# Graph layer on one core: runs grouped by ten neighbouring node tiles, with degrees, scales and parts following each group

## The chip, the cores and the metric

The kernel runs on one core of one Trainium2 chip. The metric is the device time of one execution in microseconds. Before the change it is 1150.8 us as the median of three executions (1150.80, 1148.29 and 1150.85). The profile is of one further execution, which took 1151.31 us.

TensorE multiplies matrices, VectorE and ScalarE work on rows of 128 partitions, GpSimd (POOL) here mostly issues indirect transfers, and SyncE (SP) issues plain ones. Each engine works through its own queue of instructions.

## The reference

A graph with 6250 nodes and 206250 directed edges (sorted by destination, self loops among them) is given with node features x of 256 columns.

```python
x = x + gnn(layernorm(x), edges)          # eps 1e-5
x = x + ffn(layernorm(x))

def gnn(v):                                # own loops are added once more
    deg  = segment_sum(1, dst)             # edges into each node, plus one
    dinv = 1 / sqrt(deg)
    h    = v @ W
    out  = segment_sum(h[src] * dinv[src] * dinv[dst], dst) + b
    return where(out > 0, out, a * out)

def ffn(v):                                # mixture of 8 experts, 2 chosen for the whole sequence
    ...                                    # gelu(v @ W1 + b1) @ W2 + b2, weighted, then layernorm
```

The degrees come out of the edge list, which is sorted by destination: the edges of two neighbouring nodes (a pair, one run) lie side by side.

## The kernel before

The 6250 nodes are padded to 49 tiles of 128 (NT = 49), and to 3200 pairs of neighbouring nodes (NPR). The kernel has three stages.

**The prelude** (lines 200 to 589). x is loaded in seven blocks of seven tiles (`x_load`). One h step (`h_step`) takes two tiles: four transposes on TensorE, a copy to SBUF on ScalarE (`xT`), and, one step later, eight passes of matmul with the weight, whose result ScalarE copies into `hk`. There are 25 double tiles, so 26 steps. Per-row statistics of x come from VectorE (`x_stats`, one block of seven tiles at a time), and the reciprocal root of the variance from them (`dm`, `va`, `rs`).

Meanwhile the edges are sorted into runs. A packed copy of the edge list, key and low bits of the source, goes to DRAM (`pk_d`). A coarse count (lines 324 to 337) tells where a window of 512 edges must start, `search(w)` finds the exact start of each run in it, and POOL fetches the runs with indirect transfers: 25 of them, in five groups of WP = 5 (NW = 5). Each brings one run to each of the 128 partitions. Run number c on partition p is pair 25 p + c, so group w holds pairs 25 p + 5 w to 25 p + 5 w + 4 of every partition: a group is spread over all nodes. `keys(w)` subtracts the run's base on VectorE, `turn_keys(w)` transposes on TensorE and ScalarE copies the result into `keyT` and `loT` (pair along the columns, edge slot along the partitions). `key_hots(w)` compares on VectorE and writes, interleaved, a one for each edge into the pair's first node and a one for each edge into its second node (`ev`, lines 499 and 500).

Only when all five groups are there can degrees be counted: 49 matmuls of `ev` with ones (line 545), then deg, dinv and the scale sc = rs * dinv for all 49 tiles at once. `parts(n)` then writes the scaled h of tile n as a high part (ScalarE, line 563) and the rest as a low part (VectorE, line 564) into `hp`. Three tiles' parts are placed inside each of the last six h steps, the others after h's end, among the first work of the node loop. `keep(i)` (line 784) stores seven tiles of parts to DRAM (`hl_d`) on SP.

Also in the prelude: `one_hots(u)` on VectorE makes the one-hot rows of 16 pairs from loT and keyT (lines 455), with two buffers named `unit`, which the groups of runs use as well.

**The node loop** (lines 795 to 866). For node tile n, `counts` turns one-hots into a 49 x 128 x 128 count tile `a_t` on TensorE (line 624), copied by ScalarE (line 628), and `sums` multiplies it with all 49 tiles of parts (line 644): 39 tiles this way; the last ten are summed by gathering rows of `hl_d` (lines 737 and 775). `node` and `stat` are the epilogue. Tile 0's counts and sums and tile 1's counts are written out ahead of the loop.

**Routing and the feed-forward part** (from line 929) follow the last node.

The order of the instructions on all five engines in the first two stages is the program's own (a manual schedule): an instruction waits in its queue behind those written ahead of it. SBUF is shared by slots: `s0` holds the packed edges, `s1` the loaded edges, `s2` to `s5` the blocks of x, `s6` holds `ev`; the seven blocks of parts take the same slots later.

Of the kernel before, what the change touches and what calls it, by code (L numbers as in the profile page):

```python
# [24 lines left out]
P = 128  # L25
# [9 lines left out]
def gnn_moe_kernel(  # L35
# [92 lines left out]
    WA = 3  # L128
    HG = 16
# [5 lines left out]
    assert HG * (P + PK) // 2 >= WP * P * 2  # L135
# [56 lines left out]
    with ExitStack() as ph:  # L192
# [38 lines left out]
        def x_load(i):  # L231

            if i % 2 == 0:
                x_two[0] = slots.tile([P, 2, TB, D], F32, name="xb", tag=f"s{2 + i // 2}")
            xb = x_two[0][:, i % 2]
            full = min(TB, N // P - i * TB)
            r0 = i * TB * P
            nc.sync.dma_start(
                out=xb[:, :full, :],
                in_=x[r0 : r0 + full * P, :].rearrange("(t p) d -> p t d", p=P),  # L240
            )
            for t in range(full, TB):
                for p0, r0, r in node_rows(i * TB + t):
                    nc.sync.dma_start(out=xb[p0 : p0 + r, t, :], in_=x[r0 : r0 + r, :])
            xbs[i] = xb

# [10 lines left out]
        nc.gpsimd.iota(g_i, pattern=[[1, NW], [NW, P]], base=0, channel_multiplier=0)  # L257
# [7 lines left out]
        make_identity(nc, ident_0)  # L265
        q_i = ep.tile([P, NC], I32, name="q_i")
        nc.gpsimd.iota(q_i, pattern=[[2, NC]], base=0, channel_multiplier=2 * NC)
# [150 lines left out]
        def search(w):  # L418
# [18 lines left out]
            runs[w] = unit()[:, : WP * P * 2].rearrange("p (j e f) -> p j e f", j=WP, f=2)  # L437
# [28 lines left out]
        ev = slots.tile([P, NPR, 2], BF16, name="ev", tag=f"s{NB_T - 1}")  # L466
# [11 lines left out]
        def turn_keys(w):  # L478
            key = kts.pop(w)
            s = slice(w * WP, (w + 1) * WP)  # L480
            lo = runs[w].rearrange("p j e f -> p j (e f)").bitcast(BF16)
            lo = lo.rearrange("p j (e f) -> p j e f", f=4)
            pks = [ps_k.tile([P, WP, P], BF16, name=f"pk{i}") for i in range(2)]
            for j in range(WP):
                nc.tensor.transpose(pks[0][:, j, :], key[:, j, :], ident_b)
            for j in range(WP):

                nc.tensor.transpose(pks[1][:, j, :], lo[:, j, :, 3], ident_b)
            for v, pk_ in ((keyT, pks[0]), (loT, pks[1])):
                nc.scalar.copy(  # L490
                    v.rearrange("s (p c) -> s p c", c=NC)[:, :, s],
                    pk_.rearrange("s c p -> s p c"),
                )

        def key_hots(w):
            s = slice(w * WP, (w + 1) * WP)
            k = keyT.rearrange("s (p c) -> s p c", c=NC)[:, :, s]
            e = ev.rearrange("s (p c) j -> s p c j", c=NC)[:, :, s, :]
            nc.vector.tensor_scalar(e[:, :, :, 0], k, float(NT), None, op0=OP.is_lt)
            nc.vector.scalar_tensor_tensor(  # L500
                e[:, :, :, 1], k, float(2 * NT), e[:, :, :, 0], op0=OP.is_lt, op1=OP.subtract
            )

        for i in range(2, NB_T):
            x_load(i)
        h_some(2)
# [8 lines left out]
        search(3)  # L515
        h_some(1)
        search(4)
        x_stats(2)
        h_room(1)
        hk.append((2 * HK, 1, hk2))  # L520
        h_some(2)

        dm = ep.tile([P, NT], F32, name="dm")
        va = ep.tile([P, NT], F32, name="va")
        for w in range(NW):
            keys(w)
            turn_keys(w)
            if w + 3 < NB_T:
                x_stats(w + 3)
            if w + 4 == NB_T:  # L530
                nc.vector.tensor_tensor(dm, st[:, :, 1], st[:, :, 4], OP.subtract)
                nc.vector.tensor_tensor(va, st[:, :, 2], st[:, :, 5], OP.add)
                nc.vector.scalar_tensor_tensor(dm, dm, 0.25, dm, op0=OP.mult, op1=OP.mult)
                nc.vector.scalar_tensor_tensor(va, va, 1.0 / D, dm, op0=OP.mult, op1=OP.add)
                nc.vector.tensor_scalar(va, va, LN_EPS, None, op0=OP.add)
                nc.scalar.activation(rs, va, AF.Sqrt)
            if w + 1 == NW:
                nc.vector.reciprocal(rs, rs)
            h_some(2 if w + 1 < NW else 1)
            key_hots(w)  # L540


        pdeg = pcnt[:, NW : NW + NT]
        for n in range(NT):
            nc.tensor.matmul(
                pdeg[:, n : n + 1],
                ev[:, n * P // 2 : (n + 1) * P // 2, :].rearrange("s i j -> s (i j)"), ones_b,
                start=True, stop=True, skip_group_check=True,
            )
        deg = ep.tile([P, NT], F32, name="deg")  # L550
        nc.vector.tensor_scalar(deg, pdeg, 1.0, None, op0=OP.add)
        nc.scalar.activation(dinv, deg, AF.Sqrt)
        nc.vector.reciprocal(dinv, dinv)
        nc.vector.tensor_tensor(sc, rs, dinv, OP.mult)

        def parts(n):
            i, t = divmod(n, TB)
            if t == 0:
                hp2[i] = slots.tile([P, TB, 2, D], F32R, name=f"hp{i}", tag=f"s{i}")
            h = h_at(n)[:, 0, :]  # L560
            s = sc[:, n : n + 1]
            hi, lo = (hp2[i][:, t, k, :] for k in range(2))
            nc.scalar.activation(hi, h, AF.Copy, scale=s)
            nc.vector.scalar_tensor_tensor(
                lo, h, s, hi.bitcast(F32), op0=OP.mult, op1=OP.subtract
            )

        ns = iter(range(NT))
        def some_parts(k):
            for n in itertools.islice(ns, k):  # L570
                parts(n)

        made = 0
        while h_some(1, lambda: some_parts(3)):
            made += 1
            if made in (3, 5):
                one_hots(made // 4)
# [13 lines left out]
    with main:  # L591
# [189 lines left out]
        for n in range(3):  # L781
            load(n)

        def keep(i):
            nc.sync.dma_start(
                out=hl_d[i * TB * P : (i + 1) * TB * P, :].rearrange("(t p) d -> p t d", p=P),
                in_=hp2[i].rearrange("p t k d -> p t (k d)").bitcast(F32),
            )
# [4 lines left out]


        kept, summed = 0, 0
        for n in ns:
            parts(n)
            if n % TB == TB - 1 or n == HK + 2:
                for kept in range(kept, (n + 1) // TB):
                    keep(kept)  # L800
                kept = (n + 1) // TB
            if n == HK + 2:
                counts_of(0, 0)
                counts_of(0, 1)
                one_hots(2)
            if n == HK + 5:
                counts_of(0, 2)
                one_hots(3)
            if n == HK + 7:
                counts_of(0, 3)  # L810
            if n > HK + 7:

                sums(0, summed, n)
                summed = n
# [3 lines left out]
        sums(0, summed, NT)  # L818
        for c in range(NHG):
            counts_of(1, c)  # L820
            one_hots(NHG + 2 + c) if c < 3 else None
        for g in range(3):
            g_edges(g)
# [521 lines left out]
```

## Time and profile before

| what | value |
|---|---|
| median of three executions | 1150.8 us |
| profiled execution, own time | 1151.31 us |
| its span | 1149.2 us |
| TensorE busy | 1090.8 us (95%) |
| VectorE busy | 721.5 us (63%) |
| ScalarE busy | 623.1 us (54%) |
| POOL busy | 539.0 us (47%) |
| first transposes of x | 14.03 us |
| the five groups' keys start | 41.35, 46.33, 51.70, 58.01, 64.91 us |
| all degrees on TensorE | 69.40 us |
| end of h | 82.35 us |
| first sums of tile 0 | 98.25 us |
| first counts of tile 2 (the loop) | 118.72 us |
| last sums | 765.6 us |

Times in the timeline are microseconds from the span's start, and a row names the engine, the line of the code, the operation, and the tiles written and read, followed by sizes and types. In brackets stands how long the engine sat idle ahead of the instruction and what ended that. PEclk is the share of TensorE's full clock that was granted. Busy time of an engine is not a bound by itself: an engine may be waiting in its queue while work further back in it is ready.

### The profile page before, as it was taken

To read this page: it belongs to the slowest core of one execution; us is meant where nothing else is said; L and a number is where in the kernel's file an instruction comes from. 1 tells how busy PE (TensorE), PEld (TensorE's weight loads), DVE (VectorE), ACT (ScalarE), POOL (GpSimd) and SP (SyncE) were. 2 spreads that over 40 slices of the span, in tenths; PEclk is the share of its full clock that TensorE was granted. 3 is DMA by queue.
4 is the path that set the end of the run, shared out by engine and by line. 5 is a ranking of instruction groups with operands and counts; after the bars stand their busy time and mean duration, and the time that the engine had idled before them with its cause. 6 is when DMAs were issued, how large, how long until landed. Compare 5 with 4: busy or idle time off the path is not lost. (4 is left out here: it accounts for less than half of the span.)

```text
span 1149.2 us, 17869 instructions
## 1 busy us (share of the span) xinstructions
PE 1090.8 (95%) x6552; PEld 836.3 (73%) x6552; DVE 721.5 (63%) x1523; ACT 623.1 (54%) x1529; POOL 539.0 (47%) x473
## 2 busy tenths in 40 slices
PE   6977999999999999999999999885999999999997
PEld 5766788878888888788888888763566666666666
DVE  6878876867777877777777778745333333322335
ACT  3786466766766666676667666522533333333330
POOL 3713246777767676777666766425411111100000
PEclk9997899999999999999999999886999999999999
DMA  8709637676767777677777777534011111100001
GB/s 261 237 24 343 196 86 198 160 189 172 196 172 185 179 174 182 176 180 180 184 177 177 180 182 174 140 92 140 23 37 37 37 37 37 37 19 18 19 19 37
DMA packets 102750, 152.04 MB, mean 132 GB/s; under 512 B 10047, under 2 KB 48671, under 8 KB 102655
## 3 DMA queue, kind: packets, MB, share of 16 engines
q0 software_dynamic: 54080, 99.35, 35.3%
q1 hardware_dynamic: 45378, 48.93, 13.0%
q10 hardware_dynamic: 3196, 2.55, 0.8%
q8 instruction: 53, 0.87, 0.3%
q14 instruction: 43, 0.34, 0.1%
HBM read 123.42 MB, written 27.37 MB: 131 GB/s over the span
## 5 line engine op out<-in xcount | busy, mean ns | idle before, releaser
L737 POOL DMA_INDIRECT rows<-hl_d,g_src x360 | 409.5, 1137 | 221.7 <-PE pg L775 104.6
L644 PE MATMUL po<-hp,a_t 128*128 128x512 f32 x1911 | 481.8, 402 | 0.8 <-ACT a_t L628 0.8
L644 PEld LDWEIGHTS po<-hp,a_t 128*128 128x128 f32 x1911 | 351.9, 190 | 70.2 <-ACT a_t L628 1.0
L628 ACT CAST a_t<-pa 128x392 fp32r<-128x392 f32 x624 | 257.8, 502 | 218.0 <-PE pa L624 216.5
L455 DVE TENSOR_TENSOR unit<-iota,loT 128x2048 bf16<-128x2048 bf16 x156 | 190.4, 1221 | 51.3 <-PE pa L624 51.3
L1261 PE MATMUL p<-xT,w_sb 128*128 128x512 f32 (+2 forms) x416 | 173.0, 577 | 1.6 <-ACT xT L917 1.6
L1282 PE MATMUL p<-w_sb,hT 128*128 128x256 f32 (+1 forms) x784 | 171.2, 379 | 0.0
L1282 PEld LDWEIGHTS p<-w_sb,hT 128*128 128x128 f32 (+1 forms) x784 | 147.9, 190 | 20.8 <-issue 0.9
L624 PEld LDWEIGHTS <-unit 128*128 128x128 bf16 x2496 | 124.1, 100 | 49.0 <-issue 24.8
L624 PE MATMUL pa<-unit 128*128 128x98 bf16 x2496 | 148.6, 212 | 9.5 <-DVE unit L455 5.6
L455 DVE TENSOR_TENSOR unit<-iota,keyT 128x1568 bf16<-128x1568 bf16 x156 | 150.8, 967 | 0.0
L1261 PEld LDWEIGHTS p<-xT,w_sb 128*128 128x128 f32 x416 | 79.6, 200 | 88.2 <-issue 82.9
L1287 DVE TENSOR_TENSOR yt<-yt,p 128x256 f32<-128x256 f32 (+1 forms) x49 | 20.6, 421 | 179.6 <-PE p L1282 179.6
L756 ACT ACTIVATE oh_g<-iota_f,g_dst 128x128 fp32r<-128x128 f32 x360 | 123.9, 423 | 0.0
L1265 ACT ACTIVATE hT<-p,b_sb 128x512 f32<-128x512 f32 (+2 forms) x104 | 67.3, 660 | 82.9 <-PE p L1261 82.7
L775 PE MATMUL pg<-rows,oh_g 128*128 128x512 f32 x360 | 106.0, 392 | 1.6 <-DMA rows<-hl_d,g_src 1.6
L1292 ACT ACTIVATE rs<-rs 128x1 f32<-128x1 f32 (+1 forms) x49 | 9.9, 203 | 150.0 <-DVE rs L1291 150.0
L925 POOL TENSOR_TENSOR xt<-xt,beta_bc 128x1024 f32<-128x1024 f32 (+1 forms) x13 | 29.5, 2274 | 130.0 <-DVE yt L910 130.0
L775 PEld LDWEIGHTS pg<-rows,oh_g 128*128 128x128 f32 x360 | 68.1, 189 | 18.4 <-DMA rows<-hl_d,g_src 3.7
L922 POOL TENSOR_TENSOR yt<-yt,b_sb 128x1024 f32<-128x1024 f32 (+1 forms) x13 | 29.6, 2273 | 89.7 <-PE px L915 80.4
L758 ACT ACTIVATE oh_g<-oh_g 128x384 fp32r<-128x384 f32 (+1 forms) x140 | 67.1, 479 | 4.4
L679 DVE RECIPROCAL rstd<-rstd 128x1 f32<-128x1 f32 (+1 forms) x49 | 8.0, 164 | 88.2 <-ACT rstd L678 88.2
(183 smaller groups left out, 777.1 us busy)
## 6 DMA issues: line engine op xcount, KB each, us to landing
hl_d<-hp SPq DMA_DIRECT2D x7, 1792.0 KB
x_d<-x SPq DMA_DIRECT2D x49, 128.0 KB
xt<-x_d SPq DMA_DIRECT2D x12, 512.0 KB
out_dram<-yt SPq DMA_DIRECT2D x48, 128.0 KB
rows<-hl_d,g_src POOLq DMA_INDIRECT x360, 3.8
xb<-in_x_dram SPq DMA_DIRECT2D x6, 896.0 KB
xs<-in_x_dram SPq DMA_DIRECT2D x39, 128.0 KB
xg<-in_x_dram SPq DMA_DIRECT2D x9, 128.0 KB
```

What stands on the lines that cost most here:

```text
L455: nc.vector.tensor_tensor(oh, iota2[:, :m, :].unsqueeze(1).to_broadcast([P, HG // 2, m, 2]), v[:, s].rearrange("p (q t) -> p q t", t=2).un ...
L624: nc.tensor.matmul(pa[:, i].rearrange("p j h -> p (j h)"), oh_lo[:, q, :, t], oh_key[:, q, :, t], start=True, stop=True,)
L628: nc.scalar.copy(tiles[n][:, :, b * 2 * BG : (b + 1) * 2 * BG], pa.rearrange("p i j h -> p h (i j)"),)
L644: nc.tensor.matmul(pouts[n].rearrange("p k d -> p (k d)"), tiles[n][:, g, :], hp2[g // TB][:, g % TB].rearrange("p k d -> p (k d)"), start ...
L737: nc.gpsimd.indirect_dma_start(out=g_rows[j], out_offset=None, in_=hl_d, in_offset=bass.IndirectOffsetOnAxis(ap=g_src[:, j // GC, j % GC : ...
L756: nc.scalar.activation(oh[:, i, :], iota_f, AF.Abs, bias=g_neg[:, g, c : c + 1])
L758: nc.scalar.activation(oh, oh.bitcast(F32), AF.Relu, scale=-1.0, bias=1.0)
L775: nc.tensor.matmul(pouts[n].rearrange("p k d -> p (k d)"), oh[:, i, :], g_rows.pop(g * GC + c), start=False, stop=(c == GC - 1),)
L922: nc.gpsimd.tensor_tensor(yt[:, :nt, :], yt[:, :nt, :], b2_sb.unsqueeze(1).to_broadcast([P, nt, D]), OP.add)
L1261: nc.tensor.matmul(p1[:, :cols], w1_sb[:, e, k, f * P : (f + 1) * P], xT[:, k, :cols], start=(k == 0), stop=(k == ND - 1),)
L1265: nc.scalar.activation(hT[:, e, f, :cols], p1[:, :cols], AF.Gelu, bias=b1_sb[:, e, f : f + 1])
L1282: nc.tensor.matmul(p2[:r], hT[:, e, f, t * P : t * P + r], w2_sb[:, e, f, :], start=(e == 0 and f == 0), stop=(e == TOP_K - 1 and f == NF ...
```

## The change

Group w now holds 640 neighbouring pairs: run j on partition p is pair 640 w + 5 p + j. Ten node tiles (five times 2 x 64 pairs, WT = 10) are then complete when one group is there. So degrees, scales and parts of ten tiles are computed after each group, with the next group's keys: `degrees(w - 1)` on TensorE after the turn of group w, an h step with two tiles' parts in it, `scales(w - 1)`, then `key_hots(w)`, a block's statistics, another h step with two parts. The variances' root is taken in three pieces (`x_rstd`). The comparisons now write two blocks of 64 columns side by side, so that each is a plain comparison with a constant; a degree column then holds 64 sums of first nodes and 64 of both nodes, and a small matmul with a fixed matrix (`to_node`) subtracts them and brings them into node order. The third group of runs is fetched into the unused half of the last block of x. Blocks 5 and 6 of the parts trade slots. A block of parts is stored as soon as its seven tiles are there. Behind h the counts of tile 0 are spread between the remaining parts, and eight of tile 0's sums are put between the counts of tile 1. The three first loads of edges for gathered tiles are written ahead of tile 0's counts.

```diff
-        nc.gpsimd.iota(g_i, pattern=[[1, NW], [NW, P]], base=0, channel_multiplier=0)
+        nc.gpsimd.iota(g_i, pattern=[[1, NG]], base=0, channel_multiplier=0)
...
+        to_node = ep.tile([P, P // 2, 2], F32, name="to_node")
+        nc.vector.tensor_copy(to_node[:, :, 0], ident_0[:, : P // 2])
+        nc.vector.tensor_tensor(
+            to_node[:, :, 1], ident_0[:, P // 2 :], ident_0[:, : P // 2], OP.subtract
+        )
...
-            runs[w] = unit()[:, : WP * P * 2].rearrange("p (j e f) -> p j e f", j=WP, f=2)
+            at = xbs[NB_T] if w == 2 else unit()
+            runs[w] = at[:, : WP * P * 2].rearrange("p (j e f) -> p j e f", j=WP, f=2)
...
         def key_hots(w):
-            s = slice(w * WP, (w + 1) * WP)
-            k = keyT.rearrange("s (p c) -> s p c", c=NC)[:, :, s]
-            e = ev.rearrange("s (p c) j -> s p c j", c=NC)[:, :, s, :]
-            nc.vector.tensor_scalar(e[:, :, :, 0], k, float(NT), None, op0=OP.is_lt)
-            nc.vector.scalar_tensor_tensor(
-                e[:, :, :, 1], k, float(2 * NT), e[:, :, :, 0], op0=OP.is_lt, op1=OP.subtract
-            )
+            for k in range(2):
+                nc.vector.tensor_scalar(
+                    ev[:, w, :, k, :],
+                    keyT[:, w * WN : (w + 1) * WN].rearrange("s (t q) -> s t q", q=P // 2),
+                    float((k + 1) * NT), None, op0=OP.is_lt,
+                )
...
+        def x_rstd(b0, b1):
+            t = slice(b0 * TB, b1 * TB)
+            nc.vector.tensor_tensor(dm[:, t], st[:, t, 1], st[:, t, 4], OP.subtract)
...
+            nc.scalar.activation(rs[:, t], va[:, t], AF.Sqrt)
...
+        def degrees(w):
+            t0, t1 = w * WT, min((w + 1) * WT, NT)
+            for n in range(t0, t1):
+                nc.tensor.matmul(
+                    pdeg[:, n : n + 1], ev[:, w, n - t0].rearrange("s k q -> s (k q)"), ones_b,
+                    start=True, stop=True, skip_group_check=True,
+                )
+            nc.scalar.copy(both[:, t0:t1], pdeg[:, t0:t1])
+
+        def scales(w):
+            t = slice(w * WT, min((w + 1) * WT, NT))
+            nc.tensor.matmul(
+                pnode[:, t], to_node.rearrange("p q j -> p (q j)"), both[:, t],
+                start=True, stop=True, skip_group_check=True,
+            )
+            nc.vector.tensor_scalar(deg[:, t], pnode[:, t], 1.0, None, op0=OP.add)
+            nc.scalar.activation(dinv[:, t], deg[:, t], AF.Sqrt)
+            nc.vector.tensor_tensor(sc[:, t], rs[:, t], dinv[:, t], OP.mult)
+            nc.vector.reciprocal(sc[:, t], sc[:, t])
+            nc.vector.reciprocal(dinv[:, t], dinv[:, t])
...
         search(3)
+        x_stats(2)
         h_some(1)
         search(4)
-        x_stats(2)
+        x_rstd(0, 3)
...
-        h_some(2)
+        h_some(1)
         for w in range(NW):
             keys(w)
             turn_keys(w)
+            if w > 0:
+                degrees(w - 1)
+            h_some(1, lambda: some_parts(2 if w > 1 else 0))
+            if w > 0:
+                scales(w - 1)
+            key_hots(w)
             if w + 3 < NB_T:
                 x_stats(w + 3)
...
-            h_some(2 if w + 1 < NW else 1)
-            key_hots(w)
+            if w == 1:
+                x_rstd(3, 5)
+            if w == 3:
+                x_rstd(5, NB_T)
+            h_some(1, lambda: some_parts(2 if w > 0 else 0))
+        degrees(NW - 1)
+        h_some(1, lambda: some_parts(3))
+        scales(NW - 1)
         made = 0
         while h_some(1, lambda: some_parts(3)):
             made += 1
-            if made in (3, 5):
-                one_hots(made // 4)
+            if made in (2, 4):
+                one_hots(made // 2 - 1)
...
+        for g in range(3):
+            g_edges(g)
+        counts_of(0, 0)
+        one_hots(2)
+        counts_of(0, 1)
+        one_hots(3)
+        some_parts(4)
+        counts_of(0, 2)
+        some_parts(2)
+        counts_of(0, 3)
+        summed = 0
         for n in ns:
+            if n % 2:
+                last = max(summed, min(n - 1, NT - 8))
+                sums(0, summed, last)
+                summed = last
             parts(n)
...
-        sums(0, summed, NT)
-        for c in range(NHG):
+        sums(0, summed, NT - 8)
+        counts_of(1, 0)
+        one_hots(NHG + 2)
+        counts_of(1, 1)
+        sums(0, NT - 8, NT)
+        one_hots(NHG + 3)
+        for c in range(2, NHG):
             counts_of(1, c)
             one_hots(NHG + 2 + c) if c < 3 else None
```

## The prediction

> **What bounds the kernel now.** I read the stretches of the page first, then the timeline of the first 125 us, then the granted clock in fine windows. From 300 to 600 us TensorE is busy for 299.46 of 300 us at full clock, and the feed-forward part behind it is TensorE alone; neither is touched. So the change is worth the shift of one moment: the start of the node loop, whose first counts (node tile 2) start at 118.72 us. All that follows moves with it. The timeline of the stretch before it:
>
> ```profile
> 41.35 0.81 DVE L473 TENSOR_TENSOR key<-unit,q_n 128x640 bf16<-128x640 f32 x1
> 42.71 0.90 ACT L490 COPY keyT<-pk 128x640 bf16<-128x640 bf16 x1 [0.62 <-PE pk L485]
> 43.47 0.88 ACT L490 COPY loT<-pk 128x640 bf16<-128x640 bf16 x1
> 44.37 0.75 DVE L499 TENSOR_SCALAR ev<-keyT 128x640 bf16<-128x640 bf16 x1
> 45.15 1.35 DVE L500 SCALAR_TENSOR_TENSOR ev<-keyT,ev 128x640 bf16<-128x640 bf16 x1
> 46.33 0.82 DVE L473 TENSOR_TENSOR key<-unit,q_n 128x640 bf16<-128x640 f32 x1
> 47.07 2.37 DVE L403 BATCH_NORM_STATS2 st<-xb 128x6 f32<-128x256 f32 x7
> 64.91 0.82 DVE L473 TENSOR_TENSOR key<-unit,q_n 128x640 bf16<-128x640 f32 x1 [0.70 <-DMA unit<-pk_d,r_i]
> 69.40 1.38 PE L545 MATMUL pcnt<-ones_b,ev 128*128 128x1 bf16 x49 [0.71 <-DVE ev L500]
> ...
> 75.01 0.60 PE L372 MATMUL pt<-ident_r,xb 128*128 128x128 f32 x4
> 75.91 0.59 ACT L376 COPY xT<-pt 128x512 f32<-128x512 f32 x1
> 76.39 1.32 ACT L563 ACTIVATE hp<-hk,sc 128x256 fp32r<-128x256 f32 x3
> 76.94 1.28 DVE L564 SCALAR_TENSOR_TENSOR hp<-hk,sc,hp 128x256 fp32r<-128x256 f32 x3 [0.88 <-ACT hp L563]
> ```
>
> The reader should see five groups of runs, 5.0, 5.4, 6.3 and 6.9 us apart (41.35 to 64.91, with 51.70 and 58.01 between). TensorE fills these gaps with two h steps of 2.17 us each; it is nearly full, with waits of about 1 us. VectorE's queue holds only work that is ready early, so a group waits at most for its own gather. After the last group come all degrees, six more h steps up to 82.35 us, the rest of the 49 scaled parts, and node tile 0's sums at 98.25 us. The clock in windows of 2 us, TensorE alone:
>
> ```profile
> core 0: us, PE busy (x), PEclk, DMA share, GB/s
> 82.00:84.00 2.00, 0.74 (x5) 1.00 0.00 0
> 84.00:86.00 2.00, 0.39 (x3) 0.90 0.00 0
> 86.00:88.00 2.00, 1.43 (x16) 0.50 0.15 39
> ...
> 98.00:100.00 2.00, 1.74 (x4) 0.50 1.04 375
> 100.00:102.00 2.00, 2.00 (x6) 0.50 1.05 390
> 102.00:104.00 2.00, 2.00 (x9) 0.84 1.03 376
> ```
>
> After about 3.3 us with 1.1 us of work the grant halves (85.65 us in half-microsecond windows), and it comes back only at 102.6, 4.35 us after steady work began at 98.25. Keep both figures: a short gap costs more than itself.
>
> **Parts that cost nothing.** The identity's copies for the node order (two short VectorE rows, about 0.2 us each by the cast rows around them) stand before a 2.81 us wait of VectorE for the mean's matmul. Without that cover they would cost 0.4. The third group's gather no longer waits for the first group's buffer (POOL waited 2.8 us at 43.22). At 1.25 to 1.3 us a gather, 25 of them from 28.25 end near 60, landing 1.9 us later. This gains only if keys are the late side; below they are not. SP's hl_d stores leave earlier; four now stand ahead of the bias, slope and xs loads, which nothing reads until the first node's epilogue (122.6 us in before). They start after about 70 us, when the run gathers are over, so I charge 0. The POOL order past the prelude is unchanged.
>
> **The comparisons.** Per group 0.75 plus 1.35 us (interleaved output) become two side-by-side ones. The nearest row is the 128x640 comparison at line 326, 5.05 us for 13, so 0.39 each: 0.78 instead of 2.0 start to start. Bounds are 0.25 and 0.75 each; I take 0.39 since size and 16-bit types are the same.
>
> **The new order, walked group by group.** Engines work their queues in order, so I follow VectorE, naming what it waits for. Durations, start to start, are those of the rows: key 0.82, group turn on TensorE 0.57, key copies on ScalarE 0.76 and 0.74, xT copy 0.48, a part's high half 0.40 (ScalarE), low half 0.41 (VectorE), a block's statistics 2.30, the five variance operations 1.0, degrees of ten tiles 0.25 (1.24 for 49), the scale chain 1.0 (deg, Sqrt, product, two reciprocals; 1.23 at 49 columns).
> Group 0 starts at 40.9: block 2's statistics and the first variances now stand before it, but one h step less. Key, turn, key copy, comparisons, statistics: 0.82+0.5+0.95+0.78+2.30 = 5.35. Group 1: 46.25.
> Group 1: VectorE must next write deg, behind TensorE's turn, degrees, a whole h step and the node-order matmul: 0.87+0.57+0.25+2.17+0.25 = 4.1. Then scales 1.0, comparisons 0.8, statistics 2.3, variances 1.0. ScalarE's next in line is the Sqrt of those variances, and behind it xT and the first high half (0.25+0.48+0.43+0.1); two low halves wait for these (0.8), and group 2's key stands behind them. Sum 11.3. Group 2: 57.6.
> Group 2: the low halves wait until ScalarE has made two key copies, a degree copy, xT and a high half: 0.87+0.45+2.61+0.1 = 4.0. Then 0.8 low, 1.0 scales, 0.8 comparisons, 2.3 statistics, 0.8 low: 9.75. Group 3: 67.35.
> Group 3 adds variances and their Sqrt detour (1.0+1.25): 12.0. Group 4: 79.35, against 64.91.
> From there 6.65 to the end of the comparisons (86.0), 0.3 for the degrees, and the same six h steps (70.62 to 82.35 before, 11.7): h ends at 98.0 instead of 82.35, **+15.7**.
> What comes back: 32 parts are done by then, not 18. ScalarE then has 3 parts, two small copies, 16 count copies at 0.41 and 7 parts ahead of the first sums, 11.2 us against the 15.9 (82.35 to 98.25): **-4.7**. From first sums to loop 41 sums (about 11.6, cold start as before), one count batch 0.9 and three one-hot pairs of 2.03, 18.6 against 20.5: **-1.9**. The loop's first quarter took 5.57 instead of 3.6 at a half clock; TensorE is now about 78% busy ahead of it, against 68% before that drop: **-1** (0 to -2). Together +8.1 at full clock.
> The clock: TensorE now idles 3.7, 6.0, 4.6 and 6.8 us before the turns of groups 0, 2, 3 and 4 (its own 5 us per group against the periods above). By the row each gap costs the grant, and the burst behind it runs at half speed for 4.35 us, doing 2.2 us less. Group 0's burst then ends at 48.9, 1.8 after group 1's turn is due: about 1.5. In groups 2 to 4 part hides behind ScalarE: deg would be ready at 61.7+2.2 in group 2 where VectorE comes at 62.45, so 1.5 each, plus 0.25 to 0.5 for slow turns. I take 7 in all (0 if it never drops, 10 if nothing hides).
> Sum +15 on the profiled execution's 1151.3 (span 1149.2 and 2.1 around it): 1166.4; this execution lies 0.5 above the median of 1150.8, so **1166**.
>
> The Trainium skill, "TensorE: Matmul & The Clock Gate", Part 1, says that the default is the half clock after an idle window of some 3.4 us and that a busy window of that length lifts it. It agrees with 85.65 here; by its 3.4 in place of 4.35 the clock term would be about 5.5, an estimate, and the time 1164.5. The skill's "VectorE: DVE Perf Modes", Mode 4×_2P, would let a 16-bit comparison with a constant run four elements per cycle, about 0.33 us with its overhead as an estimate; the 0.39 row shows no such rate, and the sum would move by 0.5.
>
> **Rivals.** *Same chain, clock kept* (0.20): the windows at 62 to 70 us with 68 to 85% work kept the clock in before, but none had a 4 us gap. +8: 1159.5. *Faster* (0.10): VectorE's waits do not carry from group to group, and keys come as the gathers land, some 6.2 us apart. Then group 4 starts at 64.9, h ends at 83.5, and +1.2-4.7-1.9-1 gives -6.4: 1145. Busy sums speak for it (every engine has spare time there); the queue order speaks against it. It decides if groups 1 to 4 are less than (33-8.1)/3 = 8.3 us apart on average. *Slower still* (0.12): the clock stays down through all of groups 2 to 4, or hl_d stores delay something: +20, 1171. *No effect* (0.02): hidden elsewhere; the loop's 99.8% busy TensorE excludes nearly all of it. The forecast itself has 0.56.
>
> **Range and chances.** 1156 to 1172 takes the full-clock rival with 3.5 us of error below it and most of the slowest; left out are the faster case, no effect and some 0.06 of the upper end. About 0.3% (3.5 us) is what a measurement tells here. Slower 0.87, same 0.03, faster 0.10.
>
> **What would show it.** Right: key rows about 5, 11, 10 and 12 us apart, low halves of parts waiting for ScalarE ahead of keys, TensorE idle 4 to 7 us before each turn, a grant of 0.5 between 50 and 90 us, h's end at 98 to 107, first sums soon after ScalarE's count copies, the loop's pace unchanged. Wrong: keys 6 us apart and h ending before 85.

## The result and the profile after

The changed kernel takes **1163.1 us** (median of four executions, 1161.3 to 1165.2); the kernel before took 1150.8 us beside it (four executions, 1148.3 to 1151.3). The ratio is **1.0112, 95% interval 1.0088 to 1.0135**: slower, by 12 us. The forecast was 1166 (1156 to 1172). The profiled execution took 1163.84 us, its span is 1161.9 us against 1149.2.

The timeline of the changed kernel, from the second group's key to the third's (columns: start, duration, engine, line, operation, tiles; in brackets the idle time before it and what ended that):

```profile
45.93 0.81 DVE L488 TENSOR_TENSOR key<-unit,q_n 128x640 bf16<-128x640 f32 x1
50.18 0.17 DVE L557 TENSOR_SCALAR deg<-pcnt 128x10 f32<-128x10 f32 x1 [3.45 <-PE pcnt L553]
51.20 0.50 DVE L511 TENSOR_SCALAR ev<-keyT 128x640 bf16<-128x640 bf16 x2
51.61 2.38 DVE L416 BATCH_NORM_STATS2 st<-xb 128x6 f32<-128x256 f32 x7
55.08 0.21 ACT L535 ACTIVATE rs<-va 128x14 f32<-128x14 f32 x1 [4.33 <-DVE va L534]
55.67 0.91 ACT L574 ACTIVATE hp<-hk,sc 128x256 fp32r<-128x256 f32 x2
56.21 0.88 DVE L575 SCALAR_TENSOR_TENSOR hp<-hk,sc,hp 128x256 fp32r<-128x256 f32 x2 [1.16 <-ACT hp L574]
57.01 0.82 DVE L488 TENSOR_TENSOR key<-xb,q_n 128x640 bf16<-128x640 f32 x1
57.88 0.71 PE L499 MATMUL pk<-ident_b,key 128*128 128x128 bf16 x5 [5.52 <-DVE key L488]
61.45 0.88 DVE L575 SCALAR_TENSOR_TENSOR hp<-hk,sc,hp 128x256 fp32r<-128x256 f32 x2 [3.62 <-ACT hp L574]
```

One group is a ring of waits: VectorE sits 3.45 us until TensorE has done the node-order product (`pcnt`), ScalarE sits 4.33 us until VectorE has done the variances, VectorE waits for ScalarE's high halves, and TensorE then sits 5.52 us because the next key is behind all of that in VectorE's queue. In the group after it VectorE waits 3.62 us for a high half, there with TensorE at half the clock. The table of waits of the kernel before, from 40 to 70 us (us in total, times, longest):

```profile
PEld L485 <- DVE key L473: 4.9, 5, 1.6
PE pk L485 <- DVE key L473: 3.0, 4, 1.2
DVE key L473 <- DMA unit<-pk_d,r_i: 1.8, 2, 1.1
```

and of the changed kernel, from 40 to 90 us:

```profile
PEld L499 <- DVE key L488: 19.0, 5, 5.9
PE pk L499 <- DVE key L488: 17.2, 4, 5.5
DVE hp L575 <- ACT hp L574: 12.6, 6, 3.6
ACT rs L535 <- DVE va L534: 8.8, 3, 4.3
DVE deg L557 <- PE pcnt L553: 8.2, 4, 3.5
```

The keys' waits for transfers are gone; TensorE's waits for keys went from 3.0 to 17.2 us. The clock in windows of 2 us, TensorE alone (busy us, instructions, granted clock, DMA):

```profile
core 0: us, PE busy (x), PEclk, DMA share, GB/s
40.00:42.00 2.00, 0.06 (x1) 1.00 1.10 361
54.00:56.00 2.00, 0.00 (x0) 1.00 0.35 90
58.00:60.00 2.00, 2.00 (x24) 0.50 0.44 125
64.00:66.00 2.00, 2.00 (x12) 1.00 0.00 0
72.00:74.00 2.00, 2.00 (x7) 0.50 0.28 103
82.00:84.00 2.00, 2.00 (x25) 0.50 0.00 0
88.00:90.00 2.00, 2.00 (x16) 1.00 0.00 0
```

TensorE's gaps before the turns of groups 0, 2, 3 and 4 are 3.35, 5.52, 3.08 and 5.23 us long. The last three cost the grant; the first did not. Behind h the same kernel shows:

```profile
106.12 3.21 ACT L683 CAST a_t<-pa 128x392 fp32r<-128x392 f32 x8 [2.58 <-PE pa L679]
114.84 11.29 PE L699 MATMUL po<-hp,a_t 128*128 128x512 f32 x41 [1.86 <-ACT a_t L683]
133.32 0.91 PE L679 MATMUL pa<-unit 128*128 128x98 bf16 x16 [0.68 <-DVE unit L469]
136.88 0.92 PE L679 MATMUL pa<-unit 128*128 128x98 bf16 x16
```

| moment (us) | before | after | shift |
|---|---|---|---|
| keys of the five groups | 41.35, 46.33, 51.70, 58.01, 64.91 | 41.06, 45.93, 57.01, 68.41, 80.86 | +15.95 at the last |
| end of h | 82.35 | 102.02 | +19.6 |
| first sums of tile 0 | 98.25 | 114.84 | +16.6 |
| loop (counts of tile 2) | 118.72 | 133.32 | +14.6 |
| last sums | 765.6 | 778.7 | +13.1 |
| span | 1149.2 | 1161.9 | +12.7 |

The whole loss is there when h ends, and 7 us of it come back by the end of the loop's first quarter.

One thing about the times below: in experiments 1 to 11 ScalarE and TensorE stood still for some 5 to 13 us in all, at varying points of the first 80 us, in the kernel before as well, for a reason that the profile gives only as "remote" and "issue", and the kernel before took 1168 to 1170 us there; so each ratio is to the kernel before run beside it, and distances are counted from the first key. A ratio is the record's estimate with its 95% interval; the quotient of the two medians differs from it by up to 0.2% (1.0088 in experiment 11, 1.0030 in 9), so a difference of 2 us between two ratios is not read as one.

### The profile page after: what moved, and what is told of

It reads as the page before. It is cut to its first block, busy times and chain, and to the rows that moved or that the text cites. A ratio compares the mean times of both kernels' runs of the same rounds, so it can differ in the third digit from the quotient of the medians.

```text
span 1161.9 us, 17931 instructions
## 1 busy us (share of the span) xinstructions
PE 1095.5 (94%) x6562; PEld 840.2 (72%) x6562; DVE 717.4 (62%) x1551; ACT 623.2 (54%) x1540; POOL 538.2 (46%) x473
## 5 line engine op out<-in xcount | busy, mean ns | idle before, releaser
L830 PEld LDWEIGHTS pg<-rows,oh_g 128*128 128x128 f32 x360 | 68.1, 189 | 19.2 <-DMA rows<-hl_d,g_src 4.5
```

What stands on the lines that cost most here:

```text
L830: nc.tensor.matmul(pouts[n].rearrange("p k d -> p (k d)"), oh[:, i, :], g_rows.pop(g * GC + c), start=False, stop=(c == GC - 1),)
```

## The experiments

**Theory:** the loss is the order of the queues. The scale chain and the parts of group w-1 stand ahead of the next key on VectorE, and each waits for TensorE or ScalarE, so a group takes 11 to 12 us instead of 5 to 7; the half clock adds to it. **Rivals:** the new layout or the comparisons are slow in themselves; the half clock is most of it; the parts' plain work is too much for VectorE.

**1. The same layout, the old order.** Degrees, scales and parts once, behind the last group; new comparisons, gathers and tail kept; two h steps ahead of the groups and one in the last, as before; the variances' root of blocks 3 to 6 taken once; six parts ahead of tile 0's counts, since their buffer waits for 24.

```diff
             turn_keys(w)
-            if w > 0:
-                degrees(w - 1)
-            h_some(1, lambda: some_parts(2 if w > 1 else 0))
-            if w > 0:
-                scales(w - 1)
-            key_hots(w)
             if w + 3 < NB_T:
                 x_stats(w + 3)
...
-            h_some(1, lambda: some_parts(2 if w > 0 else 0))
-        degrees(NW - 1)
-        h_some(1, lambda: some_parts(3))
-        scales(NW - 1)
+            h_some(2 if w + 1 < NW else 1)
+            key_hots(w)
+        for w in range(NW):
+            degrees(w)
+        scales()
```

> The changed kernel's layout, comparisons, third buffer and tail, but degrees and scales once for all 49 tiles after the last group, and no parts inside the groups (the order of before; six parts are added ahead of tile 0's counts, whose buffer waits for 24). Theory (the new order's queue waits are the loss): keys start about 41, 45.5, 50, 55.5 and 61.5, paced by the gathers; degrees near 66, h ends at 79 to 81, first sums near 95, time 1143 to 1148. Rival (the layout, the side-by-side comparisons or the transfers make the keys late): keys still 9 us or more apart, time 1158 or more.

Measured: 1171.65 us, ratio **1.0018** (0.9993 to 1.0044). Keys 6.7, 6.4, 5.5 and 5.0 us apart. The forecast, an absolute time beside 1150.8, meant a ratio under 1; it came out at 1. So the loss is gone with the order, and layout, comparisons and tail together neither gain nor lose within this interval. One thing that stands against a gain is visible: each batch of ten degrees on TensorE waits for ScalarE's copy of the one before, so the copies come 0.65 us apart.

```profile
82.50 0.17 ACT L549 COPY both<-pcnt 128x10 f32<-128x10 f32 x1
83.15 0.17 ACT L549 COPY both<-pcnt 128x10 f32<-128x10 f32 x1 [0.48 <-PE pcnt L545]
83.80 0.17 ACT L549 COPY both<-pcnt 128x10 f32<-128x10 f32 x1 [0.48 <-PE pcnt L545]
```

**2. The changed kernel without parts in the groups** (six more ahead of tile 0's counts).

```diff
-h_some(1, lambda: some_parts(2 if w > 1 else 0))
+h_some(1, lambda: some_parts(0))
...
-h_some(1, lambda: some_parts(2 if w > 0 else 0))
+h_some(1, lambda: some_parts(0))
```

> The changed kernel without parts inside the groups (degrees and scales stay there; 18 parts in the h steps behind, six ahead of tile 0's counts). Theory: the low halves and ScalarE's variance root no longer stand between a group's statistics and the next key, so the spacing of the keys 1 to 2, 2 to 3 and 3 to 4 falls from 11.1, 11.4 and 12.5 to about 9, 8.5 and 9.5; h ends near 93 instead of 102; 14 parts (5.7 us) come back behind h: time 1154 to 1159. Rival (low halves are only filler in time that VectorE waits anyway): spacing within 0.5 of the changed kernel's, time 1163 to 1169.

Measured: 1177.93 us, ratio **1.0085** (1.0058 to 1.0111). The forecast of 1154 to 1159 us, 1.003 to 1.007 as a ratio, was missed: keys 2 to 5 stood 10.9, 10.6 and 9.3 us apart instead of about 9, 8.5 and 9.5. From the first key to h end it took 57.25 us, against 61.0 in the changed kernel. In this order the parts are a small share: where VectorE no longer waits for high halves it waits longer for deg, though a pause of 3.4 us on TensorE may have a share in that. The table of waits of this kernel from 53 to 92 us has

```profile
DVE deg L557 <- PE pcnt L553: 14.8, 3, 6.0
```

**3. The clock held up.** The changed kernel with 9, 6 and 9 unread matmuls ahead of the turns of groups 2, 3 and 4.

```diff
             keys(w)
+            for k in range((0, 0, 9, 6, 9)[w]):
+                nc.tensor.matmul(pfill, mean_m, w_c[:, k % ND, :], start=True, stop=True)
             turn_keys(w)
```

> The changed kernel plus 9, 6 and 9 matmuls that nobody reads ahead of the turns of groups 2, 3 and 4 (about 0.47 us each), so that TensorE's gaps are filled and the clock is kept. Theory (queue waits make the gaps, the clock adds to them): no grant of 0.5 between 50 and 90 us, key 2 to key 3 falls from 11.4 to about 9.7, key 4 to degrees from 9.1 to about 7, h ends about 4 us earlier, time 1158 to 1160. Rival A (the clock is most of the loss): h ends near 87, time 1148 to 1152. Rival B (the clock costs nothing, TensorE is not waited for): no change, 1163.

Measured: 1177.71 us, ratio **1.0064** (1.0030 to 1.0098). The grant stayed at 1.00 from 60 us to h end, and the first key to h end took 56.6 us. The forecast of 1158 to 1160 us is 1.006 to 1.008 as a ratio. The interval overlaps that of the changed kernel in experiment 5 (1.0072 to 1.0152).

**4. The next key first.** Same operations; the key of group w+1 is written ahead of the scale chain and of the second pair of parts of group w, comparisons and statistics ahead of both.

```diff
+        keys(0)
+        turn_keys(0)
         for w in range(NW):
-            keys(w)
-            turn_keys(w)
+            key_hots(w)
             if w > 0:
                 degrees(w - 1)
-            h_some(1, lambda: some_parts(2 if w > 1 else 0))
-            if w > 0:
-                scales(w - 1)
-            key_hots(w)
             if w + 3 < NB_T:
                 x_stats(w + 3)
+            h_some(1, lambda: some_parts(2 if w > 1 else 0))
...
+            if w + 1 < NW:
+                keys(w + 1)
+            if w > 0:
+                scales(w - 1)
             h_some(1, lambda: some_parts(2 if w > 0 else 0))
+            if w + 1 < NW:
+                turn_keys(w + 1)
```

> The changed kernel with the same work per group in another order: the comparisons and statistics of a group come first, and the next group's key stands ahead of the scales and of the second pair of parts on VectorE, with its turn behind the second h step. Theory: the wait for the degrees and the waits for high halves are covered by the statistics; keys about 7 to 8.5 us apart, h ends at 88 to 91, first sums 12.5 us later, time 1149 to 1153. Rival (throughput of VectorE and ScalarE, not order, sets the pace): keys still 10 us or more apart, time 1158 or more.

Measured: 1173.74 us, ratio **1.0033** (1.0008 to 1.0058). Groups 9.0 (with a pause of 2.8 us on ScalarE in it), 7.2 and 8.0 us apart where the changed kernel had 11 to 12, h end 49.2 us after the first key instead of 61. Order alone, with nothing left out, takes back some 9 of 13 us. The keys are as forecast; the ratio lies above the forecast's, which was 0.998 to 1.002. What is left in an undisturbed group of it, on VectorE:

```profile
74.97 0.82 DVE L488 TENSOR_TENSOR key<-unit,q_n 128x640 bf16<-128x640 f32 x1
75.71 0.16 DVE L557 TENSOR_SCALAR deg<-pcnt 128x10 f32<-128x10 f32 x1
77.02 0.88 DVE L575 SCALAR_TENSOR_TENSOR hp<-hk,sc,hp 128x256 fp32r<-128x256 f32 x2 [0.38 <-ACT hp L574]
78.49 0.56 DVE L511 TENSOR_SCALAR ev<-keyT 128x640 bf16<-128x640 bf16 x2 [0.58 <-ACT keyT L504]
78.97 2.38 DVE L416 BATCH_NORM_STATS2 st<-xb 128x6 f32<-128x256 f32 x7
81.26 0.87 DVE L575 SCALAR_TENSOR_TENSOR hp<-hk,sc,hp 128x256 fp32r<-128x256 f32 x2
```

`deg` now starts without a wait, the longest wait is 0.58 us, and VectorE's own work fills the group.

**5. The changed kernel again**, unedited, where the experiments run.

> The changed kernel itself once more, unedited, beside the experiments, because the last four kernels ran on a chip where the kernel before took 1169.6 us instead of 1150.8. Theory (the loss is the order of the queues and the clock, not the chip): ratio to the kernel before of the same call 1.011, within 1.008 to 1.014, keys about 5, 11, 11 and 12 us apart, h ending 59 to 62 us after the first key. Rival (much of the loss hangs on how early the gathers land on that chip): a ratio below 1.005, since what is lost waiting for transfers is lost by both kernels.

Measured: 1179.33 us, ratio **1.0112** (1.0072 to 1.0152), the same as at first. Keys 5.1, 12.8, 10.4 and 12.4 us apart, h end 61.3 us after the first. The loss does not hang on those pauses. They are in the table of waits of this execution, from 20 to 60 us:

```profile
ACT hk L401 <- remote: 7.9, 1, 7.9
PE p L397 <- issue: 4.8, 2, 4.7
```

**6. The kernel before again**, one execution.

> The kernel before, unedited, for its profile on the same chip as the experiments. Theory: after its first key the same walk as in the first profile: keys 5.0, 5.4, 6.3, 6.9 us apart, degrees 28, h end 41 and node tile 0's first sums 57 us after the first key, so that the later start of all these runs is a matter of the chip's first 50 us alone. Rival (the chip is slower all over): the distances after the first key longer too, by 1% or more.

Measured: 1171.23 us. Keys 5.4, 6.9, 6.4 and 10.3 us apart, h end 50.3 us after the first key instead of 41.0. The rival's "slower all over" is not it: in the loop a matmul of the sums takes 393 ns at the median in both, and from the first counts to the last sums it takes 651.5 us against 646.9, 0.7% longer. But the forecast missed too: these pauses do not only come ahead of the first key. One of 3.7 us on ScalarE ("remote") lies between its fourth and fifth key. Single distances in experiments 1 to 11 are therefore read only where no such wait stands in the group.

**7. The variances' root later on ScalarE.**

```diff
-            nc.scalar.activation(rs[:, t], va[:, t], AF.Sqrt)
+            return t
+
+        def x_root(t):
+            nc.scalar.activation(rs[:, t], va[:, t], AF.Sqrt)
...
                 degrees(w - 1)
+            if w in (2, 4):
+                x_root(late)
...
-                x_rstd(3, 5)
+                late = x_rstd(3, 5)
```

> The changed kernel, with one instruction kind moved: the square root of the variances of blocks 3-4 and 5-6 on ScalarE stands behind the degree copy of the next group, where its operand is long ready, instead of right behind the five variance operations, where ScalarE waited 8.8 us in three waits in all. Theory (a wait in the middle of ScalarE's queue holds back VectorE's parts and through them the next key): groups 1 to 2 and 3 to 4 each shorter by 1 to 1.5 us, h end 2 to 4 us earlier after the first key than in the changed kernel, time 2 to 4 us less than it (ratio to the kernel before 1.008 to 1.010). Rival (that wait is covered by TensorE's own lateness at the half clock): key distances unchanged within 0.5 us, time the same within 1 us.

Measured: 1178.15 us, ratio **1.0099** (1.0056 to 1.0141). Keys 5.2, 11.4, 10.9 and 11.2 us apart, h end 58.4 us after the first key against 61.3. The walk is shorter by 2.9 us, as the theory has it, but the time by 1.2 us, less than its interval. Inconclusive.

**8. As 1, with degrees of groups 0 to 3 counted in the next group.**

```diff
             turn_keys(w)
+            if w > 0:
+                degrees(w - 1)
...
-        for w in range(NW):
-            degrees(w)
+        degrees(NW - 1)
         scales()
```

> The kernel with late groups (e1), but the degrees of groups 0 to 3 are counted inside the next group by TensorE and copied by ScalarE, with nothing on VectorE; the scale chain still runs once behind the last group and no parts stand in the groups. Theory (only VectorE's waits for TensorE and ScalarE cost; counting early is free and removes the four waits of some 0.5 us each between batches of ten): key distances as in e1 (6.7, 6.4, 5.5, 5.0) within 0.3 us each, last key to deg 6 to 7 us instead of 9.3, time 2 to 3 us under e1's ratio, so 0.998 to 1.000 of the kernel before. Rival (degrees inside the groups are themselves harmful): keys further apart by over 1 us in sum and h end no earlier than in e1.

Measured: 1167.88 us, ratio **1.0011** (0.9987 to 1.0035). Last key to deg 7.7 us instead of 9.3. One of the distances (10.3 us) holds a pause. That counting early is harmless is consistent with this; the expected gain of 2 to 3 us is not resolved.

**9. Keys first, six parts in the groups instead of 14, one h step more ahead of the first group and one less in the last.**

```diff
         hk.append((2 * HK, 1, hk2))
-        h_some(1)
+        h_some(2)
...
-            h_some(1, lambda: some_parts(2 if w > 1 else 0))
+            h_some(1, lambda: some_parts((0, 0, 1, 1, 2)[w]))
...
-            h_some(1, lambda: some_parts(2 if w > 0 else 0))
             if w + 1 < NW:
+                h_some(1, lambda: some_parts(1 if w > 1 else 0))
                 turn_keys(w + 1)
```

> Keys first (e4), with 6 parts in the groups instead of 14, one h step more ahead of the first group and one less in the last. In e4 the undisturbed groups stand 7.2 and 8.0 us apart, and VectorE's own work in such a group is key 0.8, scales 0.8, comparisons 0.5, statistics 2.4 and four low halves 1.75. Theory (with the waits gone, the parts on VectorE set the pace): groups 2 to 4 some 6.2 us apart in undisturbed stretches, last key to h end some 17.5 us instead of 19.9, time 5 to 7 us under e4's, a ratio to the kernel before of 0.997 to 0.999. Rival (what is left of the loss in e4 does not hang on the parts): groups still 7 us or more apart and a ratio above 1.002.

Measured: 1172.76 us, ratio **1.0049** (1.0024 to 1.0073), no better than 4: a miss. Both of the rival's conditions came true, groups of 7 us or more (7.4, 8.3 and 7.2) and a ratio above 1.002. The first two keys stood 9.0 us apart (5.1 in 4): the h step ahead came behind a late ScalarE and put the first turn at 57.5 us, 3.3 us later than in experiment 11 without that step (54.2).

**10. Keys first, no parts in the groups** (six ahead of tile 0's counts).

```diff
-            h_some(1, lambda: some_parts(2 if w > 1 else 0))
+            h_some(1, lambda: some_parts(0))
...
-            h_some(1, lambda: some_parts(2 if w > 0 else 0))
+            h_some(1, lambda: some_parts(0))
...
+        some_parts(6)
         counts_of(0, 0)
```

> Keys first (e4) without any part in the groups; 6 parts stand ahead of node tile 0's counts instead. Theory: TensorE's two h steps, turn, degrees and node-order product (4.3 + 0.9 + 0.4 + 0.3) set the pace, 6 us, so the last key is 4 us earlier than in e4; ScalarE gets 14 parts more behind it, at some 0.9 us each beside h steps or ahead of the counts, and gives 3 to 4 of it back. Ratio 1.000 to 1.003. Rival (order alone was the cause and parts are free): key distances as in e4, and a ratio of 1.004 or more since the parts come later.

Measured: 1169.08 us, ratio **0.9993** (0.9972 to 1.0013). The time is slightly better than forecast, the keys are not: the undisturbed groups are 6.4 and 6.5 us apart (7.2 and 8.0 with the parts) instead of 6, and the last key comes 2.2 us earlier after the first than in 4, not 4. The group ahead of the last key is undisturbed in 4, 9 and 10: it takes 7.98 us with four parts in it, 7.19 with two and 6.53 with none, 0.33 to 0.36 us for a part whose low half takes VectorE 0.4. So with the waits gone, the parts' plain work is what 4 still pays.

**11. The kernel of 3 again, unedited.**

> The kernel of e3 again (9, 6 and 9 unread matmuls ahead of the turns of groups 2, 3 and 4 of the changed kernel, so that TensorE does not stand idle there), with more rounds, since 1.0064 and the changed kernel's 1.0112 have intervals that touch. Theory (the half clock is worth the 7 us that were forecast, less what the extra matmuls themselves delay): ratio 1.004 to 1.008, granted clock 1.00 from the first key to h end, last key to its deg 6 to 6.5 us. Rival (the clock costs under 2 us because what it slows hides behind ScalarE): ratio 1.0095 or more.

Measured: 1179.56 us, ratio **1.0106** (1.0082 to 1.0131), above the forecast and inside the rival's bound. The grant stayed at 1.00 from 58.4 us to h end. The two do not agree well: 1.0064 and 1.0106 for the same kernel. By the profiles the first key to h end is 56.6 and 56.0 us, against 61.3 in 5, so some 5 us; by the ratios the gain is between 0.7 and 5.6 us, and the intervals overlap that of 5, so a gain of nothing is not excluded. The profiled execution, 1174.9 us, was the fastest of its six. What the half clock is worth in the time stays open.

**12. As 10, with experiment 9's h step ahead.**

```diff
         hk.append((2 * HK, 1, hk2))
-        h_some(1)
+        h_some(2)
...
-            h_some(1, lambda: some_parts(0))
             if w + 1 < NW:
+                h_some(1, lambda: some_parts(0))
                 turn_keys(w + 1)
```

> The kernel of e10 (keys first, no parts in the groups) with e9's other change: one h step more ahead of the first group, one less in the last. It tells apart which of its two changes made e9 slower than forecast. Theory A (the h step ahead: on this chip it stood behind a late ScalarE, ran at the half clock, and put the first group's turn at 57.5 us instead of 54.2): first to second key 8 to 9 us as in e9 instead of 5.2, groups 2 to 4 about 6.4 us apart as in e10, ratio to the kernel before 1.001 to 1.004. Theory B (the six parts in e9's groups): first to second key 5 to 6 us, last key to h end about 16.5 us, and a ratio of 0.997 to 0.999, which would beat the kernel before.

Measured: **1146.62 us against 1151.56 us of the kernel before beside it, ratio 0.9958 (0.9943 to 0.9972)**: 0.4% faster than the kernel before, and so faster than both. There were no pauses here. The timeline of one of its groups:

```profile
61.42 0.81 DVE L488 TENSOR_TENSOR key<-unit,q_n 128x640 bf16<-128x640 f32 x1
62.14 0.16 DVE L557 TENSOR_SCALAR deg<-pcnt 128x10 f32<-128x10 f32 x1
64.14 0.56 DVE L511 TENSOR_SCALAR ev<-keyT 128x640 bf16<-128x640 bf16 x2 [1.06 <-ACT keyT L504]
64.61 2.38 DVE L416 BATCH_NORM_STATS2 st<-xb 128x6 f32<-128x256 f32 x7
67.94 0.82 DVE L488 TENSOR_TENSOR key<-unit,q_n 128x640 bf16<-128x640 f32 x1
68.82 0.45 PE L499 MATMUL pk<-ident_b,key 128*128 128x128 bf16 x5 [1.00 <-DVE key L488]
```

TensorE waits 1.0 us for the key where it waited 3.1 to 5.5. Keys are 7.75, 6.8, 5.5 and 6.5 us apart, last key to h end 16.55 us (17.4 before). h ends at 84.5 us, still 2.1 later than before, but first sums come 15.3 us later (15.9), the loop 19.2 us after those (20.5), and the loop's first quarter takes 3.6 instead of 5.6 us: last sums 761.9 against 765.6 us. The first distance of 7.75 us is near theory A's 8 to 9; from last key to h end it is theory B's 16.5, and the ratio is slightly under theory B's. But since 9 and 10 ran with pauses and 12 without, the two changes of 9 are not separated, and how much of 12's gain over 10 is the h step is open.

## Why the prediction was right

The mechanism was that of the prediction, step by step, and its sum came out 2.5 us too high: terms on both sides were mis-sized, and part of their agreement is luck.

- **The ring of waits: right.** Forecast distances at full clock 5.35, 11.3, 9.75 and 12.0; with the forecast's clock costs (1.5 us in group 1, some 1.8 in each later group) the last three are 12.8, 11.6 and 13.8. Measured 4.9, 11.1, 11.4 and 12.45. VectorE's wait for the node-order product in group 1 was put at 3.3 us (4.1 less the key) and is 3.45; the one for high halves in group 2 at 3.1 and is 3.62, at half the clock. That the order is the cause of most of the loss is shown by 1 and 4: ratios 1.0018 and 1.0033 with the order undone or turned, against 1.0112 in 5.
- **h end: +15.7 and +7 for the clock forecast, +19.6 measured.** The full-clock walk said 98.0; h ended at 102.0. The grant was halved for 17.1 us in three stretches. Where the step failed is its size and one of its gaps: the gap before group 0 (3.35 us long) kept the clock, so the 1.5 us charged to group 1 did not occur, and group 1 took 11.1 us. Behind the other three gaps TensorE worked at half speed for 6.0, 3.4 and 6.0 us (57.88 to 63.88, 70.70 to 74.12, 81.73 to 87.77), not 4.35 each; that these make 15.4 us, near the four times 4.35 of the forecast, is luck. By the profiles of 3 and 11 the clock costs some 5 us up to h end, not 7; the ratios leave 0.7 to 5.6, and by their intervals it could be nothing.
- **The comparisons: mis-sized.** 0.39 us each was taken from another row; a pair takes 0.41 us from start to start of what follows (51.20 to 51.61), not 0.78. The Trainium skill, "VectorE: DVE Perf Modes", section "Mode 4×_2P", has four elements per cycle; the estimate of 0.33 us that the prediction worked out from it and set aside fits: the rows of `ev<-keyT` have a median of 318 ns.

```profile
L511 DVE TENSOR_SCALAR ev<-keyT x10: 262/318/327, 43.2 to 89.0; 128x640 bf16<-128x640 bf16 x10
```

  The row that was trusted has an f16 input and a different comparison value for each partition. The error helps by up to 0.37 us a group.
- **First sums after h end: -4.7 forecast, -3.1 measured.** The 11.2 us were ScalarE's own queue. The row at 106.12 shows what is missing: ScalarE waits 2.58 us for TensorE's first count, which starts 3.58 us after h's end in both kernels (85.96 and 105.60). In the kernel before, nine parts filled this time:

```profile
83.77 3.75 ACT L563 ACTIVATE hp<-hk,sc 128x256 fp32r<-128x256 f32 x9
```

  In the changed kernel none is placed there. The cover had gone with the work.
- **Sums to loop: -1.9 forecast, -2.0 measured.** Right.
- **The loop's first quarter: -1 forecast, -2.0 measured** (5.57 to 3.56 us): the clock was back in full, the better end of that term's bounds.
- **The costs put at nothing:** the identity's copies still end before a 2.68 us wait of VectorE for the mean's matmul; no key waits for a transfer; of the hl_d stores no cost is seen, but no run took them away, so that is argued only.
- **Rivals.** "Faster" needed groups under 8.3 us apart; they are 11.6 on average. "Clock kept" is excluded by the grant, which was halved for 17.1 us. "Slower still" needed the clock down through all of groups 2 to 4; it came back between them. "No effect" is excluded by the ratio.

Sum of the measured terms at the loop's first quarter: 19.6 - 3.1 - 2.0 - 2.0 = 12.5 us, against +12.7 in the span. The forecast's terms were 22.7 - 4.7 - 1.9 - 1 = 15.1.

## What to carry to other kernels

Work that can start earlier does not help if it stands in an in-order queue ahead of what feeds the next round: write the next round's feeder first, and put each dependent step where its operand is long ready (1.0112 to 1.0033 by order alone; with only the root's step moved, in 7, the gain is not resolved). Then look at the fill of the engine that carries the feeder, since plain work moved into the loop costs nearly in full once the waits are gone (0.33 to 0.36 us a part; 1.0033 to 0.9993 without them). When work is moved out of a stretch, ask which wait it had been covering.

## What the runs showed of the hardware that was not expected

- **The clock's steps lie on a fixed grid.** Quarter-microsecond windows of the changed kernel around each change of the grant:

```profile
57.00:57.25 0.25, 0.00 (x0) 0.60 1.37 262
63.75:64.00 0.25, 0.25 (x4) 0.74 0.00 0
70.50:70.75 0.25, 0.25 (x4) 0.91 0.00 0
74.00:74.25 0.25, 0.25 (x4) 0.76 1.01 385
80.75:81.00 0.25, 0.00 (x0) 0.89 0.00 0
87.75:88.00 0.25, 0.25 (x4) 0.96 0.00 0
```

  From the share of each window at full clock the changes are at 57.05, 63.88, 70.70, 74.12, 80.94 and 87.77 us: 2, 2, 1, 2 and 2 times 3.41 us apart. So the half-clock stretches in these rows last 3.4 or 6.8 us, not 4.35. The stretch from 70.70 had work throughout its first 3.41 us and ended after them; those from 57.05 and 80.94 began with 0.8 us without work and went on for another 3.41. In all fourteen profiles every change of the grant from 20 to 135 us lies on such a grid within 0.02 us; where the grid lies differs from execution to execution. Whether a gap costs the grant therefore hangs on where it falls and not on its length alone. The first row below is the changed kernel's, the others are experiment 12's:

```profile
41.94 0.45 PE L499 MATMUL pk<-ident_b,key 128*128 128x128 bf16 x5 [3.35 <-DVE key L488]
42.32 2.58 PE L397 MATMUL p<-w_sb,xT 128*128 128x256 f32 x8 [2.96 <-ACT xT L389]
43.50:43.75 0.25, 0.25 (x2) 0.69 0.50 160
```

  The gap of 3.35 us left 1.46 us of work between the grid points at 39.99 and 43.40, and the clock was kept. The shorter one of 2.96 us left 1.28 us between 40.18 and 43.60, and the clock was lost at 43.60. How much work is enough is not shown: the kernel before lost the grant at 116.30 with 1.94 us of it in the 3.41 us ahead. The Trainium skill, "TensorE: Matmul & The Clock Gate", Part 1, has a free-running window of 3413 ns; these rows agree with it.
- **ScalarE's copy of 128x640 from PSUM takes 0.69 us instead of 0.90** when it writes 640 neighbouring columns instead of five out of each 25 (`keyT` and `loT`, the same input pattern).
- **Pauses of 5 to 13 us in all on ScalarE and TensorE** in experiments 1 to 11, with no releaser that the profile shows. Their cause was not found.
